# Unread matrix products in TensorE's estimated gaps, and new estimates for the order of a two-layer decoder

## The chip, the core and the metric

The kernel runs on one core of one Trainium2 chip. The metric is the device time of one execution in microseconds, the median of several. A core has five engines with an instruction stream each: TensorE (PE: matrix products and transposes), VectorE (DVE), ScalarE (ACT), GpSimd (POOL) and SyncE (SP, which only issues transfers here). Each works through its own stream in order and waits for the others through semaphores.

## The reference, cut to what matters

The input is `x`, 4 sequences of 256 tokens with 256 features: 1024 tokens in all. Six blocks are added to it in turn, each behind a layer normalisation:

```
x = x + L0_attn(norm(x))            # linear attention with a decay, 16 heads
x = x + L0_xattn(norm(x), itok, ctx)  # 4 experts chosen by token id, weights from ctx
x = x + L0_ffn(norm(x))             # product-key memory: 8 heads x 8 rows out of a table of 2048
x = x + L1_attn(norm(x))            # causal 3-tap convolution, attention inside blocks of 16, 8 heads
x = x + L1_xattn(norm(x), ctx)      # 16 heads over all 1024 context tokens, quantised to 8 bits
x = x + L1_ffn(norm(x))             # one shared and 16 routed experts, 2 for each token
```

In `L0_ffn` each token picks 64 rows of the table (8 heads of 8), forms a weight for each from the row's first 128 values, and adds the rows' other 256 values under these weights. In `L1_xattn` a softmax over 1024 keys is formed for every token and head and its probabilities are rounded to 8 bits.

## The kernel before

The tokens are 8 tiles of 128 (`xt[0]` to `xt[7]`). Work is written as Python generators, "streams", each of which yields the engine that it will need next. Their steps are woven into one order for TensorE, ScalarE and VectorE by hand-made estimates, while the program is built; on the chip nothing is decided any more.

- `Clock.note` (line 79) gives each instruction an estimated cost and keeps for each engine the time at which it is free. `Clock.weave` (line 111) takes, out of the streams that could start within `NEAR` = 0.6 us of the earliest, the one with the highest lead.
- `Slots` (line 155 on) counts PSUM buffers: `take` waits until one is free, `give` returns it. [...]In the first part `accs` has one bank and `f` (`bank`, line 348) seven; later `accs` has one, `sc` four (two buffers of two banks), `tp` one and `mm` two.

The streams are these.

- `front(b)`, b = 0 to 3 (pairs of tiles): the first three blocks up to the choice of table rows. Its products go into `f`.
- `fetches` (line 609): for each tile 8 steps of 8 indirect DMAs by GpSimd, which gather table rows into `g` (three buffers): 512 gathers.
- `weigh` (line 620): for each of the 64 steps, VectorE multiplies and sums `g`, ScalarE takes a tanh, VectorE writes the weights into `blk`, and TensorE adds the rows with 8 products of 32 columns into `accs[:, 0, :]`. When these are through, the buffer of `g` is free for the gathers three steps on.
- `locals_`: for each pair of tiles the fourth block and the queries of the fifth. `routes`: the router and the shared expert of the sixth. Both use `mm`.
- `units(k, 3)`, three streams at a time (line 943): the cross attention of one tile and head, 128 units in all. One unit is two products of 512 columns into `sc`, a maximum on VectorE, an exponential on ScalarE into 8-bit `e`, two transposes into `tp`, a cast on ScalarE from `tp` into `qqT`, and eight products of 16 columns into `accs[:, 1, :]` (`accs<-vi,qqT` in the profile).

After the weave come the routed experts (31 slots of 128 rows, lines 1195 to 1231) and the gathering of their results. That part is written without `Clock`.

All instructions that go through `Clock` stand in the profile under line 75, so they are told apart by the names of their tiles.

Of the kernel before, what the change touches and what calls it, by code (L numbers as in the profile page):

```python
# [11 lines left out]
F32 = mybir.dt.float32  # L12
BF16 = mybir.dt.bfloat16
# [8 lines left out]
P = 128  # L22
D = 256
# [28 lines left out]
class Clock:  # L52
# [26 lines left out]
    def note(self, engine, op, out, args, kw):  # L79
        if engine == "sync":  # L80
            return
        n = math.prod(out.shape[1:])
        if engine == "tensor":
            moved = args[2] if op == "matmul" else args[1]
            wide = moved.dtype == F32
            cost = 0.04 + n * ((0.0016 if op == "matmul" else 0.0022) if wide else 0.00085)
            if out.shape[0] == 32:
                cost = 0.115
        elif engine == "scalar":
            cost = 0.2 + n * 0.00083 + (0.2 if "accum_out" in kw else 0)  # L90
        elif engine == "gpsimd":
            cost = 1.25
        elif op in ("max", "max_index", "tensor_reduce"):
            src = args[1] if op != "max_index" else args[2]
            cost = 0.16 + 0.00104 * math.prod(src.shape[1:]) + (0.05 if op == "max_index" else 0)
        elif op == "reciprocal":
            cost = 0.1 + 0.0064 * n
        elif op == "tensor_tensor_scan":
            cost = 0.16 + 0.0022 * n
        else:  # L100
            cost = 0.16 + (0.00054 if op in ("tensor_scalar", "tensor_copy") else 0.00104) * n
        if self.last not in (None, engine):
            self.t = self.end + self.HOP
        start = max(self.free[engine], self.t)
        self.free[engine] = start + cost
        self.end = max(self.end, start + cost)
        self.last = engine
# [3 lines left out]
    def weave(self, streams):  # L111

        live = self.live = list(streams)
        while live:
            able = []
            for s in live:
                t = s.t
                engine, wait = s.wait  # L120
                if isinstance(wait, Slots):
                    if not wait.left:
                        continue
                    t = max(t, wait.at)
                elif wait is not None:
                    at = wait()
                    if at is None:
                        continue
                    t = max(t, at)
                able.append((max(t, self.free[engine]), t, s))  # L130
            first = min(x[0] for x in able)
            _, t, s = max((x for x in able if x[0] <= first + self.NEAR), key=lambda x: (x[2].lead, -x[1]))
            self.lead = s.lead
            self.t = self.end = t
            self.last = None
            try:
                s.wait = next(s.gen)
            except StopIteration:
                live.remove(s)
                s.done = self.end  # L140
            s.t = self.end + self.HOP

    def fork(self, *gens):

        made = [Stream(g, self.lead, self.end + self.HOP) for g in gens]
        self.live.extend(made)
        yield "vector", lambda: max(s.done for s in made) if all(s.done is not None for s in made) else None
# [8 lines left out]
class Slots:  # L156
# [7 lines left out]
    def take(self, shape, dtype=F32):  # L164
        while not self.left:
            yield "tensor", self
        self.left -= 1
        return self.pool.tile(shape, dtype, name=self.tag, tag=self.tag, bufs=self.n)

    def give(self):  # L170
# [4 lines left out]
def decoder(ctx, tc, a, out):  # L175


    nc = tc.nc
    ck = Clock(nc)
# [6 lines left out]
    A = SimpleNamespace(turned=None)  # L186
# [38 lines left out]
    ident = base.tile([P, P], F32, name="ident", tag="ident")  # L225
    make_identity(nc, ident)
    identb = base.tile([P, P], BF16, name="identb", tag="identb")
# [44 lines left out]
    psp = psum_ctx.enter_context(tc.tile_pool(name="psp", bufs=1, space=PSUM))  # L272
    psf = front_ctx.enter_context(tc.tile_pool(name="psf", bufs=1, space=PSUM))
# [2 lines left out]
    accs = psp.tile([P, 2, D], F32, name="accs", tag="accs")  # L276
    nc.vector.memset(accs, 0.0)

    blk = []
# [63 lines left out]

    hdram, pT, idxT, known = {}, {}, {}, {}
    fronts_left = [NB]
    bank = Slots(ck, psf, "f", 7)

    def front(b):  # L350
        tiles = (2 * b, 2 * b + 1)
# [591 lines left out]
    def units(k, n):  # L943

        work = A.work
        for j in range(k, NT * XH, n):
            t, h = j // XH, j % XH
            yield "tensor", lambda: qready.get(t)
            o, c = h % 2, h // 2
            hr = slice(o * 64, o * 64 + 64)  # L950
            psc = yield from A.sc.take([P, T])
            for n_ in range(2):
                te_.matmul(psc[:, n_ * 512:(n_ + 1) * 512], QT[t][hr, c, :], kT[hr, c, n_ * 512:(n_ + 1) * 512],
                           start=True, stop=True)
            yield "vector", None
            mx = work.tile([P, 1], F32, name="mx", tag="mx", bufs=4)
            ve_.tensor_reduce(mx, psc, AX.X, ALU.max)
            nb = work.tile([P, 1], F32, name="nb", tag="nb", bufs=4)
            ve_.tensor_scalar(nb, mx, NSQ[t][:, h:h + 1], ln255, ALU.mult, ALU.add)
            yield "scalar", None  # L960

            e = work.tile([P, T], U8, name="e", tag="e", bufs=3)
            se_.activation(e, psc, AF.Exp, bias=nb, scale=SQ[t][:, h:h + 1], accum_out=SUMS[t][:, h:h + 1])
            A.sc.give()
            yield "tensor", None

            tp = yield from A.tp.take([P, 2, P])
            for o in range(2):
                te_.transpose(tp[:, o, :], e.bitcast(F32)[:, o * P:(o + 1) * P], ident)
            yield "scalar", None  # L970
            qqT = work.tile([P, 8, P], BF16, name="qqT", tag="qqT", bufs=3)
            se_.copy(qqT.rearrange("p (o j) q -> p o j q", o=2), tp.bitcast(U8).rearrange("p o (q j) -> p o j q", j=4))
            A.tp.give()

            yield "tensor", lambda: 0.0 if t == 0 else summed.get(("o", t - 1))
            for s in range(NT):
                te_.matmul(accs[:, 1, h * XD:(h + 1) * XD], qqT[:, s, :], vi[:, s, h * XD:(h + 1) * XD],
                           start=False, stop=(s == NT - 1), skip_group_check=True)
            nunits[t] += 1
            if nunits[t] == XH:  # L980
                summed[("x", t)] = ck.end
# [147 lines left out]
    with tc.manual_schedule(engines={mybir.EngineType.PE, mybir.EngineType.Activation, mybir.EngineType.DVE}):  # L1129
        ck.weave([*[Stream(follow(b), 5.0 - b, (0.0, 20.0, 0.0, 0.0)[b]) for b in range(NB)],  # L1130
                  Stream(keys_values(), 0.5, 25.0), Stream(fetches(), 20.0), Stream(weigh(), 6.0),
                  Stream(turn()), Stream(weights()), Stream(locals_(), 1.5),
                  *[Stream(after_turn(units, k, 3), 2.0) for k in range(3)],
                  Stream(cross_out(), 3.0), Stream(routes(), 1.0)])
# [46 lines left out]
    for tj in range(NT * 2):  # L1181
# [3 lines left out]
                         start=(tj == 0), stop=(tj == NT * 2 - 1))  # L1185
# [115 lines left out]
def build(arrays):  # L1301
    import concourse.bacc as bacc

    nc = bacc.Bacc("TRN2", target_bir_lowering=False, num_devices=1)
    a = {k: nc.dram_tensor(f"in_{k}", v.shape, mybir.dt.from_np(v.dtype), kind="ExternalInput").ap()
         for k, v in arrays.items()}
    out = nc.dram_tensor("out_0", (T, D), F32, kind="ExternalOutput").ap()
    with tile.TileContext(nc) as tc, ExitStack() as ctx:
        decoder(ctx, tc, a, out)
    return nc  # L1310
# [9 lines left out]
```

## Time and profile before

| | us |
|---|---|
| three runs | 1367.18, 1361.3, 1358.31 (median 1361.3) |
| the profiled execution, whole | 1457.97 |
| its span, first to last instruction | 1456.2 |
| TensorE busy, granted clock over the span | 897.2 (62%), 0.659 |
| VectorE, ScalarE, GpSimd busy | 847.4, 519.3, 570.2 |
| first and last start of a gather (`g<-in_table`) | 126.4, 919.7 |
| first and last start of a unit's exponential (`e<-sc`) | 685.1, 1282.4 |

The profiled execution is 7% longer than the median of the runs, so times of the profile are set against its own span. "Clock" is the share of full speed that TensorE was granted. A busy time of TensorE is modelled, and work in flight overlaps. A row of the trace is one recorded instruction: an fp32 product leaves two of them, a bf16 product or an fp32 transpose one.

### The profile page before, as it was taken

How to read it: one execution, taken by the hardware profiler on the slowest of the kernel's cores; microseconds unless marked ns; L12 is line 12 of the kernel's file. 1: busy time of each engine (PE TensorE's matmuls, PEld its weight loads, DVE VectorE, ACT ScalarE, POOL GpSimd, SP SyncE). 2: the span in 40 equal slices, each digit the busy share in tenths (PEclk: the TensorE clock that was granted, in tenths of full speed). 3: DMA queues.
4: the chain of work that ended last, by engine and by line, in shares of the span. 5: the costliest groups of instructions: out<-in, count | busy, mean ns of one | idle time of the engine just before them, and what ended most of it. 6: DMA issues, size and time to landing. Idle time of an engine off the chain costs nothing.

```text
span 1456.2 us, 15280 instructions
## 1 busy us (share of the span) xinstructions
PE 897.2 (62%) x4829; PEld 530.4 (36%) x4829; DVE 847.4 (58%) x2309; ACT 519.3 (36%) x1039; POOL 570.2 (39%) x584
## 2 busy tenths in 40 slices
PE   4881561376624812645867664787679767756992
PEld 3670440154402500432333242444345443333551
DVE  6849476857775568246657557655654566533222
ACT  1341220122201301122555513668375838731220
POOL 1004676666667676646666656200000000002324
PEclk8995675588856855655655565755665565556996
DMA  5012577666667688855766657330000000003323
GB/s 173 0 34 75 145 172 179 163 172 171 179 180 181 175 243 216 198 147 142 179 170 173 166 152 176 100 124 0 8 0 0 1 8 1 1 8 73 89 71 102
DMA packets 93165, 165.56 MB, mean 114 GB/s; under 512 B 14858, under 2 KB 65275, under 8 KB 93084
## 3 DMA queue, kind: packets, MB, share of 16 engines
q0 software_dynamic: 35024, 106.86, 24.7%
q1 hardware_dynamic: 58060, 57.72, 18.7%
q8 instruction: 39, 0.64, 0.2%
q14 instruction: 42, 0.34, 0.1%
HBM read 157.85 MB, written 6.68 MB: 113 GB/s over the span
## 4 chain that ended last, share of the span: by engine, by line
PE 35%; DVE 25%; issue 15%; ACT 12%; DMA 5%; POOL 4%; another core or an unknown queue 3%; DVEq 0%; ACTq 0%; POOLq 0%
PE mm L75 11%; PE f L75 7%; PE accs L75 5%; ACT e L75 4%; ACT qqT L75 4%; POOL g L75 4%; DVE mx L75 3%; PE sc L75 3%; DMA g<-in_table,idxT 3%; PE ph L1211 3%; PE tp L75 3%; DVE g L75 2%; DVE z L75 2%; DVE oh L75 2%
## 5 line engine op out<-in xcount | busy, mean ns | idle before, releaser
L75 POOL DMA_INDIRECT g<-in_table,idxT x512 | 519.3, 1014 | 394.3 <-issue 146.9
L75 DVE TENSOR_REDUCE mx<-sc 128x1 f32<-128x1024 f32 x128 | 156.4, 1222 | 126.1 <-PE sc L75 107.3
L75 PE MATMUL accs<-g,blk 128*32 128x256 f32 x1024 | 110.6, 573 | 172.6 <-DVE blk L75 105.2
L1202 POOL DMA_INDIRECT xr<-xs,smap x31 | 29.3, 945 | 459.5 <-DVE smap L1189 402.4
L75 ACT ACTIVATE e<-sc,nb,qs_q 128x1024 uint8<-128x1024 f32 x128 | 154.2, 1205 | 69.5 <-DVE nb L75 62.2
L75 ACT CAST qqT<-tp 128x1024 bf16<-128x1024 uint8 x128 | 129.0, 1007 | 79.0 <-PE tp L75 56.9
L75 PE MATMUL sc<-kT,qT 64*128 64x512 bf16 x256 | 121.9, 585 | 31.0 <-ACT e L75 26.6
L75 PE MATMUL tp<-ident,e 128*128 128x128 f32 x256 | 83.4, 427 | 73.1 <-ACT qqT L75 45.0
L75 PEld LDWEIGHTS accs<-g,blk 128*32 128x32 f32 x1024 | 35.6, 147 | 225.2 <-DVE blk L75 120.8
L75 PEld LDWEIGHTS tp<-ident,e 128*128 128x128 f32 x256 | 35.8, 195 | 146.0 <-ACT qqT L75 75.9
L75 DVE TENSOR_TENSOR g<-g,hb 128x1024 f32<-128x1024 f32 x64 | 78.3, 1224 | 12.6 <-DMA g<-in_table,idxT 7.1
L75 DVE TENSOR_REDUCE z<-g 128x8 f32<-128x1024 f32 x64 | 78.1, 1220 | 3.0 <-issue 0.4
L75 PEld LDWEIGHTS <-qqT 128*128 128x128 bf16 x1024 | 48.2, 109 | 60.6 <-ACT qqT L75 32.5
L75 ACT ACTIVATE th<-u 128x8 f32<-128x8 f32 x64 | 13.3, 207 | 153.5 <-DVE u L75 85.4
L75 DVE SCALAR_TENSOR_TENSOR blk<-th,u 64x8 f32<-64x8 f32 x128 | 21.5, 168 | 69.1 <-ACT th L75 39.9
L75 PE MATMUL accs<-vi,qqT 128*128 128x16 bf16 x1024 | 49.7, 178 | 14.4 <-ACT qqT L75 8.6
L75 ACT ACTIVATE ln_xn<-x,ln_nmr,ln_rstd 128x256 f32<-128x256 f32 x48 | 26.3, 592 | 86.8 <-DVE ln_nmr L75 74.0
L1211 PE MATMUL ph<-w,xrT 128*128 x124 | 48.9, 507 | 0.7 <-DVE xrT L1208 0.6
L1215 DVE TENSOR_TENSOR hd<-hd,ph 128x176 f32<-128x176 f32 x31 | 10.4, 338 | 63.2 <-ACT hd L1214 63.2
L75 PE MATMUL f<-ident,ix 128*128 128x128 f32 x8 | 3.6, 450 | 64.6 <-DVE sm L75 51.4
L75 PE MATMUL f<-ident,ln_xn 128*128 128x128 f32 x48 | 12.1, 382 | 45.3 <-ACT ln_xn L75 18.5
L75 DVE TENSOR_SCALAR nb<-mx,nsq,ln 128x1 f32<-128x1 f32 x128 | 34.9, 273 | 8.4 <-DVE mx L75 0.5
(290 smaller groups left out, 1737.5 us busy)
## 6 DMA issues: line engine op xcount, KB each, us to landing
hb<-hdram SPq DMA_DIRECT2D x128, 256.0 KB
g<-in_table,idxT POOLq DMA_INDIRECT x512
w<-in_w SPq DMA_DIRECT2D x16, 352.0 KB
ys<-yr SPq DMA_DIRECT2D x31, 128.0 KB
w_w2a<-in_w SPq DMA_DIRECT2D x1, 2048.0 KB
x<-in_x SPq DMA_DIRECT2D x8, 128.0 KB
w_ctxT<-in_ctxT SPq DMA_DIRECT2D x1, 1024.0 KB
w_w_up<-in_w_up SPq DMA_DIRECT2D x1, 1024.0 KB
```

What stands on the lines that cost most here:

```text
L75: return emit(*args, **kw)
L1202: nc.gpsimd.indirect_dma_start(out=xr, out_offset=None, in_=xs, in_offset=bass.IndirectOffsetOnAxis(ap=smap[:, i:i + 1], axis=0))
L1211: nc.tensor.matmul(ph.rearrange("p j n -> p (j n)"), xrT[:, k, :], w13[:, bass.ds(e, 1), k, :], start=(k == 0), stop=(k == 1))
L1215: nc.vector.tensor_tensor(hd, hd, ph[:, 1, :], ALU.mult)
```

## The change

- The estimates for TensorE in `Clock.note` become smaller; an instruction of GpSimd is put at 1.3 instead of 1.25 us.
- A tile `spare`, one PSUM bank, is added beside `accs`. `keep_busy` is called before each step that begins on TensorE: where the estimated idle time of TensorE is over 0.3 us, it writes up to 24 products of 256 columns in bf16 (`identb` against `ident` read as bf16) into the first half of `spare`, one for each 0.16 us. They are not entered in the estimates. Nothing reads them.
- For this bank, `f` has six buffers instead of seven. Later the transposes of `e` go into the second half of `spare`; `take(None)` then only counts the one `tp` slot and makes no tile.

```diff
--- before.py
+++ after.py
@@ -83,13 +83,13 @@
         if engine == "tensor":
             moved = args[2] if op == "matmul" else args[1]
             wide = moved.dtype == F32
-            cost = 0.04 + n * ((0.0016 if op == "matmul" else 0.0022) if wide else 0.00085)
+            cost = max(0.14 if wide else 0.05, 0.03 + n * (0.0009 if wide else 0.00045))
             if out.shape[0] == 32:
-                cost = 0.115
+                cost = 0.08
         elif engine == "scalar":
             cost = 0.2 + n * 0.00083 + (0.2 if "accum_out" in kw else 0)
         elif engine == "gpsimd":
-            cost = 1.25
+            cost = 1.3
@@ -131,6 +131,8 @@
             first = min(x[0] for x in able)
             _, t, s = max((x for x in able if x[0] <= first + self.NEAR), key=lambda x: (x[2].lead, -x[1]))
             self.lead = s.lead
+            if s.wait[0] == "tensor":
+                self.keep_busy(max(t, self.free["tensor"]) - self.free["tensor"])
             self.t = self.end = t
             self.last = None
@@ -140,6 +142,15 @@
+    IDLE = 0.3
+    filler = None
+
+    def keep_busy(self, gap):
+
+        if self.filler is not None and gap > self.IDLE:
+            for _ in range(min(int((gap - 0.1) / 0.16), 24)):
+                self.filler()
+
@@ -165,6 +176,8 @@
         while not self.left:
             yield "tensor", self
         self.left -= 1
+        if shape is None:
+            return None
         return self.pool.tile(shape, dtype, name=self.tag, tag=self.tag, bufs=self.n)
@@ -275,6 +288,9 @@
     accs = psp.tile([P, 2, D], F32, name="accs", tag="accs")
     nc.vector.memset(accs, 0.0)
+
+    spare = psp.tile([P, 2, D], F32, name="spare", tag="spare")
+    ck.filler = lambda: nc.tensor.matmul(spare[:, 0, :], identb, ident.bitcast(BF16), start=True, stop=True)
@@ -345,7 +361,7 @@
-    bank = Slots(ck, psf, "f", 7)
+    bank = Slots(ck, psf, "f", 6)
@@ -964,7 +980,8 @@
-            tp = yield from A.tp.take([P, 2, P])
+            yield from A.tp.take(None)
+            tp = spare[:, 1, :].rearrange("p (o q) -> p o q", o=2)
             for o in range(2):
                 te_.transpose(tp[:, o, :], e.bitcast(F32)[:, o * P:(o + 1) * P], ident)
             yield "scalar", None
```

## The prediction

> **What bounds the kernel now.** I read the page first, then the busy time in six stretches, then the chain of waits, then single rows at both clocks.
>
> ```profile
> span 1456.2 us, 15280 instructions
> PE 897.2 (62%) x4829; PEld 530.4 (36%) x4829; DVE 847.4 (58%) x2309; ACT 519.3 (36%) x1039; POOL 570.2 (39%) x584
> PEclk8995675588856855655655565755665565556996
> PE 35%; DVE 25%; issue 15%; ACT 12%; DMA 5%; POOL 4%; another core or an unknown queue 3%; DVEq 0%; ACTq 0%; POOLq 0%
> ```
>
> No engine is full. TensorE holds the largest share of the chain (35%), and its clock sits at five to six tenths from slice 12 to slice 34. A faster clock is worth something only in that 35%.
>
> ```profile
> 0.00:137.00 137.00, 79.55 (x354) 64.15 (x354) 97.73 (x355) 36.98 (x74) 14.67 (x33) 0.84 0.21 65
> 137.00:600.00 463.00, 222.35 (x1263) 142.37 (x1263) 304.77 (x971) 81.60 (x194) 312.01 (x306) 0.67 0.72 183
> 600.00:921.00 321.00, 199.29 (x1224) 105.60 (x1224) 188.59 (x382) 129.18 (x261) 199.08 (x198) 0.58 0.64 162
> 921.00:1296.00 375.00, 283.39 (x1572) 154.87 (x1568) 207.60 (x429) 241.50 (x409) 0.00 (x0) 0.58 0.06 20
> 1328.00:1456.00 128.00, 96.99 (x368) 54.48 (x368) 34.15 (x108) 26.61 (x93) 40.61 (x43) 0.87 0.31 86
> ```
>
> The columns are the busy times of PE, PEld, DVE, ACT and POOL, then the clock, the DMA share and GB/s. I call the first four stretches A (fronts before the gathers), B and C (gathers, with fronts, then with attention), D (attention after the last gather). In B and C GpSimd paces: a gather takes 0.95 us and 0.30 us of issue, so 512 need 640 of the 784 us from 137 to 921. Of the rest, the view of `accs` puts 79.7 us down to buffers that TensorE frees late. In D TensorE is the fullest engine (283 of 375 us, against 242 for ScalarE), and the chain of that window says the same:
>
> ```profile
>   POOL g L75: 79.7, 21
> by line: PE mm L75 26.2%; ACT e L75 13.3%; ACT qqT L75 12.9%; PE sc L75 8.7%; PE tp L75 8.0%; DVE mx L75 6.1%; issue 5.1%; PE accs L75 3.0%; DVE q L75 1.7%; DVE ln_nt L75 1.4%; DVE nb L75 1.4%; ACT pr L75 1.3%; DVE x L75 1.1%; DVE ln_st L75
> ```
>
> The same work at both clocks (start, length, engine, operation), half clock first:
>
> ```profile
> 149.01 1.94 PE L75 MATMUL accs<-g,blk 128*32 128x256 f32 x16 [5.16 <-DVE blk L75]
> 928.79 1.07 PE L75 MATMUL accs<-g,blk 128*32 128x256 f32 x16
> 970.14 1.03 PE L75 MATMUL sc<-kT,qT 64*128 64x512 bf16 x2
> 921.05 0.59 PE L75 MATMUL sc<-kT,qT 64*128 64x512 bf16 x2
> 975.41 0.69 PE L75 MATMUL tp<-ident,e 128*128 128x128 f32 x2
> 927.10 0.44 PE L75 MATMUL tp<-ident,e 128*128 128x128 f32 x2
> ```
>
> Doubling the clock K takes these to 0.55 to 0.64 of their time; a unit's eight `accs<-vi,qqT` stay near 0.4 us. I write TensorE's time as proportional to 0.2 + 0.4/K: 0.89 at K = 0.58, 0.83 at 0.63, 0.77 at 0.7, 0.67 at 0.85, 0.6 at 1.
>
> **What the Trainium skill says.** "TensorE: Matmul & The Clock Gate", Part 1, says that the array runs at half clock unless it was busy for a window of about 3.4 us. The trace agrees: every stretch that I took out had 1.00 or 0.50 and nothing between, in multiples of 3.4 us. The same page, "Back-to-back issue gap", prices a bf16 product of N columns at N/1.2 ns cold and N/2.4 + 2.5 ns warm. So one added product is put at 213 ns cold and 109 ns warm, 0.126 us at K = 0.85, an estimate from that page; the trace has no such product. "PSUM — Partial Sum Buffer", Terms, says that two engines must not use the same bank at once. No run here shows a collision, but it matters for `spare`, where the added products and the casts' source share a bank.
>
> **What counts as busy.** From 960 to 1000 us TensorE is busy 31.1 of 40 us and the clock is 0.50; from 40 to 80 us it is busy 32.4 and the clock is 0.96. So busy time alone doesn't decide. I tallied columns streamed in each 3.4 us window (fp32 records twice; products on 64 rows half, on 32 columns a quarter, `accs<-vi,qqT` nothing, weights chosen to fit which windows are followed by full clock). Full speed follows about 4000 from cold, and stays above about 3400. Stretch means: A 3950 (clock 0.84), B 2650 (0.67), C 2210 (0.58), D 2300 (0.58), 1296 to 1440 us 4060 (0.85).
>
> **The change, part by part.**
>
> The order of TensorE's instructions after the change has 2622 added products in 284 runs: 286 before the first `accs<-g`, 1070 from there to the first `sc`, 667 from there to the last `accs<-g`, 599 behind it. Over the 1160 us from 137 to 1296 that is 2336 products, 598,000 columns, or 1760 in each 3.4 us. With it the means become 4410 in B, 3970 in C and 4060 in D. By A and the tail, such means go with about 0.85. I take K = 0.85 in B, C and D.
>
> The new estimates move work. At the last `accs<-g` the order before has emitted 45 units and 261 products or transposes into `mm`; the order after 64 and 335. So 19 units and 74 `mm` instructions leave D for B and C, where ScalarE was free (129 of 321 us in C).
>
> D: TensorE keeps 64 of 83 units and 215 of 290 `mm` instructions, about 76% of its work: 283 x 0.76 = 215 us. At K = 0.85, x 0.67/0.89 = 162. Added: 599 x 0.126 = 75. Sum 237. At today's filling (283/375 = 0.755) D lasts 314 us: 61 us less.
>
> A flaw keeps D from being shorter. In 98 runs (544 products) the first added product carries a wait for ScalarE: it shares the bank that the cast to `qqT` reads. 56 of them stand ahead of `accs<-vi,qqT` and 38 ahead of the next transposes, which need that same cast too. There the added products fill no gap; they start when the work behind them could start, 5.6 (544/98) x 0.126 = 0.7 us each. That is why I leave the filling at 0.755 and don't raise it.
>
> B and C: TensorE had 222 + 199 = 421 us. It takes over 19 units at 2.1 us (1.03 + 0.69 + 0.41) = 40, and 74 x 0.45 (131 us for 290 `mm` instructions in D) = 33: 494 us. At K = 0.85, x 0.67/0.83 = 399. Added: 1737 x 0.126 = 219. Sum 618 of 784 us: 79% full instead of 54%. Its products for `weigh` come behind more, and on these GpSimd waits. Of the added ones 831 stand in 58 runs straight ahead of `accs<-g`: 14.3 each, 1.8 us. Where TensorE waited for `blk` (26 groups, 105 us, 4 us each) they fit. In the other 38 they delay: 68 us, of which a third reaches GpSimd, as today 21 of 64 do: +23. The faster groups themselves (1.94 to about 1.2 us, 64 times, a third) give back 15. The third part, fuller queues, is not in the trace; between -10 and +60, taken as +12. B and C: +20 us.
>
> A: 286 products, mostly ahead of transposes that wait for a layer normalisation, and a clock already at 0.84: 0, from -5 to +10. Six buffers of `f` instead of seven: 0 to +10, taken as 0, since TensorE's own speed frees them sooner. TensorE's program grows by 2622 loads and 2622 products; ScalarE once waits 16.1 us for an unknown queue in B, which may be instructions; 0 to +15, taken as 0. The tail is untouched at 0.87.
>
> Sum: -61 + 20 = -41 on 1457.97, so 1417. The median of the runs stands at 1361.3/1457.97 = 0.934 of the profiled execution: -38, so 1323 us.
>
> **The rivals.**
>
> Full effect: K = 1 in D and the gathers at their own pace. D: 215 x 0.6/0.89 + 599 x 0.109 = 210, /0.755 = 278, 97 less; B and C 10 less. -107 x 0.934: 1261 us. For it: full clock persists once 3400 columns are kept up. Against: the runs are bursts, and TensorE's waits for `blk` last up to 17 us.
>
> The gathers give it back: as D shrinks by 61, B and C grow by 60, because 79% filling in order delays most `accs<-g`. For it: 79.7 us of waits are there already. Against: GpSimd has three buffers. 1361 us.
>
> Slower: the clock stays near 0.7, because bursts of 4 to 7 products don't fill a window, and the added products become load instead of warmth. 0.155 us each. B and C: 494 x 0.77/0.83 + 1737 x 0.155 = 727 of 784 us, 93% in order; the gathers stretch by some 50. D: 215 x 0.77/0.89 + 599 x 0.155 = 279, /0.755 = 369, nothing gained. +50 x 0.934: 1408 us. It decides from K below about 0.77, where D's gain (some 30 us) no longer covers the gathers' loss. For it: the threshold from cold is nearly a full window. This is also the case in which the change doesn't do what it says.
>
> **How the numbers follow.** Forecast 0.42 (1323; alone 1295 to 1347), full effect 0.13, given back 0.20, slower 0.25. Below 1270 lies half of the full effect; above 1410 nearly half of the slower case; so 1270 to 1410. About 1% is what a measurement of this kernel can tell. Faster by over 1%: nearly all of the forecast, the full effect, a fifth of the given-back case: 0.57. Within 1%: three fifths of that case, a little of its neighbours: 0.16. Slower: 0.27.
>
> **What would show it.** The clock should read about 0.85 from 137 us on and the mean over the span over 0.8; at 0.7 the slower case holds. The last gather should start near 940 us, with about 60 exponentials before it; over 970 means that it was given back. The stretch from the last gather to the end of the units should last near 315 us. In it `accs<-vi,qqT` should wait behind added products after the cast. A span near 1415 us fits; over 1475 it is wrong.

## The result: slower by 6.6%, and the gathers end 98 us later

| | before | after |
|---|---|---|
| median of the runs, us | 1362.5 | 1453.0 |
| ratio, 95% interval | | 1.066 (1.0625 to 1.070) |
| profiled execution: span, clock | 1364.3, 0.665 (second profile) | 1452.6, 0.804 |

The forecast was 1323 us, range 1270 to 1410: it expected a gain, and the time came out above the range. Ratios leave out executions over 1.5% longer than the fastest of their kernel; medians hold all of them.

First a correction to what the prediction stood on. Its profile of the kernel before (span 1456.2) is of an execution that the runs don't resemble. A second profile of the same kernel has a span of 1364.3 us, and from here on "before" means that one. The two differ in one place: the last gather starts at 920 us in the first and at 826 in the second; from there to the first read of the routed experts (`xr`) it is 403 and 405 us, behind it 133 and 133.

The page after: TensorE busier, its clock up, as wished. The lines are the span, the engines' busy times and the clock in 40 slices.

```profile
span 1452.6 us, 20511 instructions
PE 1138.4 (78%) x7451; PEld 757.6 (52%) x7451; DVE 846.0 (58%) x2309; ACT 524.9 (36%) x1039; POOL 575.1 (40%) x584
PEclk8997998999997879756598978885656855577996
```

Busy time by stretch, cut at the last gather and at the first `xr`; columns PE, PEld, DVE, ACT, POOL, clock, DMA share, GB/s. Before (second profile), then after:

```profile
0.00:137.00 137.00, 79.58 (x354) 64.07 (x354) 97.59 (x355) 36.98 (x74) 14.67 (x33) 0.84 0.22 65
137.00:600.00 463.00, 244.74 (x1454) 156.36 (x1454) 333.68 (x1030) 97.92 (x246) 351.72 (x339) 0.68 0.81 201
600.00:826.00 226.00, 161.95 (x1037) 82.24 (x1034) 161.65 (x326) 115.24 (x210) 164.57 (x166) 0.58 0.75 192
826.00:1231.00 405.00, 300.48 (x1617) 165.86 (x1616) 220.75 (x490) 243.47 (x417) 0.60 (x1) 0.57 0.07 21
1231.00:1364.00 133.00, 98.09 (x372) 54.88 (x372) 34.78 (x110) 27.72 (x94) 44.46 (x47) 0.86 0.31 86
```

```profile
0.00:137.00 137.00, 105.13 (x576) 86.39 (x577) 95.32 (x351) 37.30 (x74) 14.49 (x33) 0.88 0.21 65
137.00:600.00 463.00, 369.81 (x2662) 269.21 (x2661) 344.09 (x1059) 112.01 (x264) 336.05 (x323) 0.89 0.76 193
600.00:924.00 324.00, 257.95 (x1910) 156.48 (x1909) 191.78 (x359) 160.09 (x294) 179.05 (x182) 0.77 0.58 147
924.00:1320.00 396.00, 307.93 (x1937) 190.85 (x1934) 180.14 (x434) 188.05 (x316) 1.12 (x1) 0.68 0.08 21
1320.00:1452.00 132.00, 97.55 (x372) 54.68 (x372) 34.72 (x109) 27.48 (x94) 44.39 (x47) 0.87 0.31 86
```

The gathers end 98 us later; the attention behind them is only 9 us shorter although it holds 65 units instead of 88; nothing else moves. Of the 98 us, 84 fall on the last three of the eight tiles of gathers, while attention units are under way: these tiles take 134, 104 and 107 us, where before they took 85, 85 and 91. GpSimd's waits for buffers that TensorE frees (view of `accs`, us and times) went from the first line to the second:

```profile
  POOL g L75: 14.3, 11
  POOL g L75: 106.2, 26
```

In the attention the added products stand where they hurt. From the timeline after (start, length; in brackets the idle time before and what ended it):

```profile
999.53 1.01 ACT L75 CAST qqT<-spare 128x1024 bf16<-128x1024 uint8 x1 [0.98 <-PE spare L75]
...
1000.59 1.23 PE L293 MATMUL spare<-ident,identb 128*128 128x256 bf16 x5 [1.16 <-ACT qqT L75]
...
1001.61 0.63 PE L75 MATMUL spare<-ident,e 128*128 128x128 f32 x2
...
1002.04 1.06 PE L293 MATMUL spare<-ident,identb 128*128 128x256 bf16 x4
...
1002.89 0.40 PE L75 MATMUL accs<-vi,qqT 128*128 128x16 bf16 x8
1003.13 1.01 ACT L75 CAST qqT<-spare 128x1024 bf16<-128x1024 uint8 x1 [1.28 <-PE spare L293]
...
1003.23 1.03 PE L75 MATMUL sc<-kT,qT 64*128 64x512 bf16 x2
...
1004.30 1.23 DVE L75 TENSOR_REDUCE mx<-sc 128x1 f32<-128x1024 f32 x1 [3.84 <-PE sc L75]
```

The cast (`CAST`) reads the second half of `spare`, and the added products write its first half. TensorE sits idle for 1.16 us while the cast runs, the very gap that the five products were meant for. They start when the cast has ended, and the next transposes wait behind them. Four more follow these; the next cast reads the same bank and starts at 1003.13, when they are through. The next `sc` is late, and VectorE has been idle for 3.84 us. `spare` is one tile and one bank, so no run here tells for which of the two the wait is placed; below, both are called the bank.

### The profile page after: what moved, and what is told of

Same layout as the page of the kernel before. It is cut to its first block, busy times and chain, and to the rows that moved or that the text cites. A ratio compares the mean times of both kernels' runs of the same rounds, so it can differ in the third digit from the quotient of the medians.

```text
span 1452.6 us, 20511 instructions
## 1 busy us (share of the span) xinstructions
PE 1138.4 (78%) x7451; PEld 757.6 (52%) x7451; DVE 846.0 (58%) x2309; ACT 524.9 (36%) x1039; POOL 575.1 (40%) x584
## 5 line engine op out<-in xcount | busy, mean ns | idle before, releaser
L293 PE MATMUL spare<-ident,identb 128*128 128x256 bf16 x2622 | 418.2, 317 | 116.0 <-ACT qqT L75 114.1
L293 PEld LDWEIGHTS <-identb 128*128 128x128 bf16 x2622 | 288.0, 112 | 227.2 <-issue 162.9
L75 ACT CAST qqT<-spare 128x1024 bf16<-128x1024 uint8 x128 | 129.3, 1010 | 163.5 <-PE spare L75 142.4
L75 PE MATMUL accs<-g,blk 128*32 128x256 f32 x1024 | 83.5, 453 | 54.7 <-DVE blk L75 54.6
L75 PE MATMUL sc<-kT,qT 64*128 64x512 bf16 x256 | 104.7, 513 | 7.4 <-ACT e L75 7.2
L75 PEld LDWEIGHTS accs<-g,blk 128*32 128x32 f32 x1024 | 30.1, 123 | 89.7 <-DVE blk L75 63.2
L75 PE MATMUL spare<-ident,e 128*128 128x128 f32 x256 | 72.8, 379 | 3.3 <-ACT qqT L75 2.9
L75 PEld LDWEIGHTS spare<-ident,e 128*128 128x128 f32 x256 | 37.8, 184 | 57.5 <-issue 39.9
```

Source lines behind the costliest of these rows:

```text
L75: return emit(*args, **kw)
L293: ck.filler = lambda: nc.tensor.matmul(spare[:, 0, :], identb, ident.bitcast(BF16), start=True, stop=True)
```

## The experiments

All are read by their medians and by the ratio to the kernel before on the same chip. The first twelve ran on chips where that takes 1362 to 1365 us, the last six on chips where it takes 1464 to 1466; times of the two sets are not compared by microseconds.

### The kernel before, again

No edit.

> The kernel before, unchanged, for a profile of an execution that lasts as long as its timed runs (its first profile was 7% longer than they are). Theory A (the first profile was an unusual execution, with long waits for an unknown queue during the gathers): the span is near 1362 us, the last gather starts near 830 us instead of 920, and the clock is near 0.66. Theory B (the timed runs have a warmer TensorE): the span is near 1362 us with a clock of 0.75 or more. Theory C: the profile lengthens this program, and the span is near 1456 us again with timed runs near 1362.

1363.8 us; span 1364.3, clock 0.665, last gather at 826 us, and no waits for an unknown queue: theory A. The eight tiles of gathers take 85 to 91 us each, where the first profile had 95 to 108.

### No products

```diff
-    IDLE = 0.3
+    IDLE = 1e9
```

> The changed kernel with IDLE at 1e9, so that no added product is emitted; new estimates, spare and six buffers of f stay, and all other instructions stand in the same order. Theory P (the added products are load, and half of them stand behind the cast that the next work waits for): the loss of 91 us goes with them, 1340 to 1370 us. Theory O (the order from the small estimates is at fault): it stays slow, 1420 us or more. Theory W (the warmth pays and the order costs even more): slower still than 1453 us.

1383.2 us, ratio 1.017 (1.0115 to 1.022). Between the theories: the order alone, with six buffers of `f`, costs 21 us, the products the other 70. The stretch of the gathers and the attention behind it:

```profile
137.00:897.00 760.00, 473.98 (x2842) 275.47 (x2842) 537.13 (x1416) 272.70 (x560) 511.87 (x503) 0.64 0.73 180
897.00:1249.00 352.00, 227.19 (x1271) 122.81 (x1271) 178.40 (x429) 184.89 (x312) 0.86 (x2) 0.58 0.09 24
```

The gathers end 71 us later than before (826 to 897) and the rest up to the first `xr` is 53 us shorter (405 to 352). The gathers stretch although TensorE is busy for only 474 of 760 us. GpSimd's waits for buffers that TensorE frees:

```profile
  POOL g L75: 90.0, 33
```

### Products, but the old estimates

```diff
-            cost = max(0.14 if wide else 0.05, 0.03 + n * (0.0009 if wide else 0.00045))
+            cost = 0.04 + n * ((0.0016 if op == "matmul" else 0.0022) if wide else 0.00085)
...
-                cost = 0.08
+                cost = 0.115
...
-            cost = 1.3
+            cost = 1.25
```

> The changed kernel with the estimates of before, so that the order of all else is that of before; 1710 added products instead of 2622, in the gaps of the old estimates. Theory P: the loss falls with the number of products, some 60 us over before, near 1420 us. Theory O: the loss goes, 1340 to 1370 us.

1385.2 us, ratio 1.020 (1.014 to 1.025). Neither figure was met. In this order 43 runs with 232 products wait for a cast, where the changed kernel has 98; shared out, the 23 us of loss are 0.5 us for each of the 43.

### No products in the time of the cast

```diff
-        if self.filler is not None and gap > self.IDLE:
+        if self.filler is not None and gap > self.IDLE and self.casting is None:
...
                 te_.transpose(tp[:, o, :], e.bitcast(F32)[:, o * P:(o + 1) * P], ident)
+            ck.casting = j
...
+            if ck.casting == j:
+                ck.casting = None
             nunits[t] += 1
```

> The changed kernel, but no products are added between a unit's two transposes and its eight products behind the cast, so that none waits for ScalarE: 1970 instead of 2622 are left. Theory P in its form that the shared bank costs (each such run delays the chain by some 0.7 us and drags the cast): 60 us or more come back, below 1395 us. If the products cost only as load, a quarter of the loss goes, about 1430 us. Theory O: no change, 1453 us.

Here `casting` holds a unit from its two transposes until its eight products behind the cast; 652 of the 2622 products go. 1383.1 us, ratio 1.017 (1.012 to 1.023): 70 us come back, to the time without any product. So the products of the cast's time cost 70 us, and the other 1970 together nothing on balance. In the lines below the gathers end at 892 instead of 924 us and the attention takes 351 instead of 396.

```profile
137.00:892.00 755.00, 604.25 (x4261) 395.69 (x4258) 536.52 (x1414) 273.00 (x559) 512.78 (x503) 0.81 0.71 181
892.00:1243.00 351.00, 256.76 (x1578) 147.61 (x1578) 178.50 (x429) 184.39 (x312) 0.82 (x2) 0.64 0.09 25
```

Beside the kernel without products the clock is up from 0.64 to 0.81 where GpSimd's gathers and their waits set the time, but only from 0.58 to 0.64 in the attention, where TensorE's speed was expected to count.

### The old estimates, and no products in the time of the cast

The edits of the last two together.

> The estimates of before (the order of all other instructions is that of before) with 1448 added products, none between a unit's transposes and its products behind the cast. Theory P (only the products behind the cast cost; the rest is free): the 23 us that the old order with 1710 products lost come back, 1355 to 1365 us. If the warmer clock pays at all in this order: below 1350 us, faster than both kernels. Theory L (every added product costs as load): 1375 us or more.

1361.6 us, ratio 0.999 (0.997 to 1.001), clock 0.760. The 23 us are back, and 1448 products change nothing: gathers 84 to 90 us a tile, 402 us of attention at a clock of 0.62.

### One product in the time of the cast

```diff
-            for _ in range(min(int((gap - 0.1) / 0.16), 24)):
+            for _ in range(min(int((gap - 0.1) / 0.16), 24 if self.casting is None else 1)):
```

> The changed kernel, but between a unit's transposes and its products behind the cast a run has one added product instead of four or more: 2098 in all, 98 runs still wait for the cast. If the work of these products costs (some 0.7 us for each run on the path): most of the 70 us comes back, 1385 to 1405 us. If the wait that they carry is what costs: 1440 us or more.

`casting` is set as in "No products in the time of the cast". 1393.3 us, ratio 1.023 (1.018 to 1.028). The 98 waits are still there and cost about 10 us with one product each. It is the work started after the wait that costs: from the first product of such a run to the next other work of TensorE it is 96.0 us in all in the changed kernel, and 15.9 here.

### A bank for each, against a shared one

```diff
-        A.mm = Slots(ck, A.ps, "mm", 2)
+        A.mm = Slots(ck, A.ps, "mm", 1)
...
-            yield from A.tp.take(None)
-            tp = spare[:, 1, :].rearrange("p (o q) -> p o q", o=2)
+            tp = yield from A.tp.take([P, 2, P])
```

The first hunk alone makes the shared kernel, both make the one with a bank for each. Both have 2794 products in the same places.

> One buffer of mm instead of two frees a bank: the transposes of e go back to a bank of their own and the added products (2794, also those of the time of the cast) have theirs. Read only against the next kernel, which has the same order of instructions. Theory P: 60 us or more below it, since the products then run while the cast runs. If the products cost as load alone: within 15 us of it.

> One buffer of mm instead of two, all else as in the changed kernel: transposes and added products share a bank, 95 runs wait for the cast. With one buffer of mm slower than 1453 us. Theory P: 60 us or more above the kernel with a bank for each; load alone: within 15 us of it.

A bank for each: 1370.7 us, ratio 1.004 (1.002 to 1.0055). Shared: 1463.3 us, ratio 1.072 (1.067 to 1.077). The same products in the same order cost 93 us more for the bank alone. With two buffers of `mm`, as in the changed kernel, no bank is left for this, so there it was not tried. Who waits for the tile `spare` (us, times), shared, then own; the transposes write `spare` only in the shared kernel, so the last line gives the casts' waits for `tp` in the other:

```profile
  ACT qqT L75: 145.7, 95
  PE spare L293: 103.5, 85
```

```profile
  PEld f L75: 2.4, 2
  POOL g L75: 0.6, 2
```

```profile
  ACT qqT L75: 76.9, 69
```

The products' own waits for the cast are gone, and the casts wait about half as long.

### A bank for each, without products

On top of both hunks:

```diff
-    IDLE = 0.3
+    IDLE = 1e9
```

> The kernel with one buffer of mm and a bank for each, without any added product, in the same order: what the warmer clock is worth. If warmth pays: 20 to 50 us above the 1371 us of the kernel with 2794 products. If it doesn't: within 10 us of it.

1440.7 us, ratio 1.055 (1.051 to 1.059): products with a bank of their own are worth 70 us in this order. The two stretches without products, then with them:

```profile
137.00:896.00 759.00, 467.63 (x2728) 269.48 (x2728) 518.75 (x1391) 252.32 (x513) 515.65 (x503) 0.64 0.73 180
896.00:1306.00 410.00, 276.09 (x1386) 144.18 (x1385) 196.30 (x453) 205.53 (x359) 0.72 (x1) 0.52 0.07 21
```

```profile
137.00:862.00 725.00, 594.45 (x4550) 407.12 (x4549) 522.20 (x1394) 252.59 (x514) 507.21 (x502) 0.90 0.76 188
862.00:1237.00 375.00, 309.77 (x2127) 195.48 (x2125) 192.63 (x451) 204.13 (x357) 1.19 (x2) 0.79 0.08 23
```

Half of it (34 us) comes ahead of the last gather, half (35) behind it; there the clock goes from 0.52 to 0.79. So here a warmer clock pays, also ahead of the last gather, where with two buffers of `mm` it didn't; why is not shown. The order with one buffer of `mm` takes the gain back: without products it is some 55 us slower than the order with two (1440.7 against 1383.2), which is itself 21 us slower than before.

### A bank for each, with the old estimates

> Products in a bank of their own (one buffer of mm), with the estimates of before: 1959 products, none waits for a cast. If the order from the new estimates is what keeps the kernel with a bank for each at 1371 us: faster than before, 1330 to 1350 us. If gathers set the pace and warmth has nothing left to give: 1355 to 1370 us.

1393.3 us, ratio 1.021 (1.018 to 1.024): both theories missed. The gathers run at full pace (83 to 91 us a tile, last one at 819 us), but only 34 units are started by then, and the rest takes 436 us with one buffer of `mm`.

### One estimate at a time

The kernel before with only GpSimd's estimate changed (1.25 to 1.3), and with only TensorE's.

> The kernel before with only the estimate of a GpSimd instruction changed, 1.25 to 1.3 us (54 instead of 45 units ahead of the last weighing). The new estimates together cost 21 us. If work pulled ahead of the weighing is what delays the gathers: about half of that, 1370 to 1378 us, with the last gather 20 to 40 us later. If the estimates of TensorE are what matters: 1362 us.

> The kernel before with only TensorE's estimates changed (61 units ahead of the last weighing), two buffers of mm, seven of f, no spare. If pulled work is what delays: most of the 21 us, 1375 to 1385 us, with the last gather 40 us or more later. If the GpSimd estimate or the lost buffer of f is what matters: 1362 us.

GpSimd's alone: 1336.3 us, ratio 0.978 (0.974 to 0.981): faster than both kernels, and not as expected. TensorE's alone: 1363.0 us, ratio 0.999 (0.997 to 1.001). A line of the trade for each order, all without products:

| order | last gather, us | units started by then | from there to the first `xr`, us | median, us |
|---|---|---|---|---|
| before | 826 | 40 | 405 | 1362 |
| GpSimd's estimate | 832 | 49 | 374 | 1336 |
| TensorE's estimates | 862 | 53 | 370 | 1363 |
| both (six buffers of `f`) | 897 | 63 | 352 | 1383 |

In these four orders, the more units stand ahead of the last gather, the shorter the rest. Nine more than before come nearly free for the gathers (7 us); with 13 and 23 more they pay 36 and 71 us, as much as the rest saves and more. The orders differ in more than this count, so it is a fit of four points and not shown as the cause.

### What the other chips left open

These six runs are three kernels, each run twice, on chips where the kernel before takes 1464 to 1466 us. The first is the kernel with the old estimates and no products in the time of the cast, with GpSimd's estimate at 1.3. The second is the kernel before with all new estimates and nothing else. The third is the kernel with a bank for each, without products in the time of the cast.

> GpSimd's estimate at 1.3 us, TensorE's estimates of before, and 1433 added products of which none stands between a unit's transposes and its products behind the cast. The estimate alone gave 1336 us. If products outside the cast's time are neutral, as they were twice: 1330 to 1342 us. If warmth pays in this order: below 1330 us. If they cost as load: above 1345 us.

> The same kernel as e13 (GpSimd's estimate at 1.3 us, 1433 products, none during a cast), on a chip of the usual speed if it falls so. Products neutral: 1330 to 1342 us, as GpSimd's estimate alone (1336). Warmth pays: below 1330. Load: above 1345. On the slow chip: 0.985 to 0.995 of before, as e13.

0.990 (0.9845 to 0.995) and 0.992 (0.990 to 0.995), slightly faster than before here too; the medians of all runs, 1457.7 and 1455.4 us, are 0.994 of before. Whether the products add to GpSimd's estimate or take from it isn't shown, since that estimate alone ran on no such chip.

> The kernel before with all new estimates and nothing else: seven buffers of f, no spare, no products. The same order as the changed kernel without products (1383 us), which has six buffers of f. If the lost buffer of f costs the 21 us: 1360 to 1366 us. If the two estimates together make the worse order: 1378 to 1388 us, with the last gather near 895 us.

> The same kernel as e14 (all new estimates on the kernel before, seven buffers of f). If the lost buffer of f costs the 21 us: 1360 to 1366 us. If the two estimates together make the worse order, for which the 1.009 of the slow chip speaks: 1375 to 1388 us, with the last gather near 895 us.

1.0087 (1.006 to 1.012) and 1.009 (1.0055 to 1.013): slower with seven buffers of `f`. So the two estimates together make the worse order; whether the lost buffer adds to the 21 us stays open.

> One buffer of mm, a bank for each, 2202 products: those of the time of the cast are left out (2794 with them gave 1371 us, none at all 1441 us). If the products during the cast are what keeps the clock up in the attention: 1400 to 1440 us, with the clock after the last gather falling from 0.79 to about 0.65. If with one buffer of mm any warmth pays: within 15 us of 1371 us.

> The same kernel as e15 (one buffer of mm, a bank for each, no products during a cast). If the products during the cast carry the clock in the attention: 1400 to 1440 us, for which its clock of 0.68 after the last gather on the slow chip speaks. If any warmth pays: within 15 us of 1371 us.

1.037 (1.033 to 1.040) and 1.046 (1.041 to 1.051). The stretch behind the last gather in the first and the second:

```profile
1016.00:1400.00 384.00, 284.63 (x1802) 161.58 (x1801) 195.87 (x453) 205.40 (x359) 1.06 (x2) 0.68 0.08 23
998.00:1385.00 387.00, 288.32 (x1814) 163.25 (x1813) 195.99 (x453) 205.65 (x359) 0.59 (x1) 0.68 0.08 22
```

This stretch differs little between the two sorts of chip (403 and 405 us in the two profiles of before), so it may be set beside the other two kernels of this order: 410 us and clock 0.52 without products, 375 us and 0.79 with all. By that, the products outside the casts bring 23 to 26 of the 35 us, and those in the time of the cast the rest and the step from 0.68 to 0.79. It is one comparison across chips and no proof.

## Why the prediction was wrong, by its own steps

- **The gathers: the step that failed first.** "B and C: +20 us." The whole change stretched them by 98 us, and the new order alone, without one added product, by 71. The term of the sum that was too small is "fuller queues", "between -10 and +60, taken as +12". It was the only place for what the moved work does to the weighing, and this came out above the whole range. In the kernel without products GpSimd's waits for buffers grew from 14.3 to 90.0 us, 64.9 of them in the last three tiles of gathers. TensorE was not full there (474 of 760 us), so its fullness was the wrong measure. Which engine's order holds the weighing up isn't shown: in those tiles VectorE also waits 26.7 us for ScalarE's tanh. The +23 us for products ahead of `accs<-g` did not show: with the products outside the casts the gathers end at 892 us, without any at 897.
- **The room in the first profile.** Its stretch of 784 us held 79.7 us of waits, where an execution like the timed ones has 689 us and 14.3. The forecast of TensorE's load was good (618 us, measured 628), but in 689 us that would have been 90% full, not 79%.
- **The shared bank: named, and put at nothing.** The prediction saw the 98 runs that wait for the cast and priced them at 0.7 us each, but they entered the sum only as a filling not raised above 0.755, in D. Measured: 70 us for the products of the cast's time. Of the 76 us between the two profiled spans 45.7 fell in D and 31.5 in the gathers. Shared out over the runs this is 0.71 us, and that it meets 0.7 is in part luck: each run held up TensorE's next work by 0.98 us in the mean (96.0 in 98 runs), and not all of this reached the end. It also left out that the next cast waits in turn for products emitted ahead of it.
- **The order.** Forecast: D shrinks by 61 us, from the order, the clock and the added products together. The new order alone shortened it by 53 us at an unchanged clock. That the two are near is luck: by the prediction's own figures the order alone gives 375 - 215/0.755 = 90. The unit count (64 of 128 ahead of the last weighing) came out as 63 started.
- **The clock.** Forecast: 0.85 from 137 to 1296 us, over 0.8 in the mean. Measured 0.89 and 0.77 in the gathers, 0.68 behind them, 0.804 in the mean: right for the first part, too high for the last, where it was to pay. The sum spread the 2336 products evenly, 1760 columns in each 3.4 us; by its own count only 599 of them stand in D, about 1400, and D also gives away a quarter of its own columns. Counted as the prediction does, by the start of each record, B, C and D had 5200, 3600 and 3100 columns, not 4410, 3970 and 4060. The threshold of 4000 from cold doesn't come out of such a count either. In both profiles of before, the one after and the one with a bank for each, up to the first `xr`, half clock followed 689 of the 698 windows of 3.4 us with under 2800 columns, and full clock 566 of the 578 with 3600 or more, with the clock at half or at full alike; in between it went either way.
- **The price of a product.** Forecast 0.126 us. TensorE was busy with them for 418.2 us, 0.160 each, but this holds the modelled end of the last one of each of the 284 runs. From start to start within a run it was 0.139 us in the mean, and from 0.109 in the median to 0.213 for the slow tenth: the two prices that the prediction had taken.
- **The scale.** The factor 0.934 spread the 7% of the first profile over all stages. The second profile has all of it in the gathers.
- **The rivals.** "The gathers give it back" had the right place, at +60 where the order alone made +71, and no price for the bank on top. "Slower" named a clock near 0.7 and products that are only load. In D the clock was 0.68, but that is not what cost: without the products of the cast's time it was 0.64 there, and D was 45 us shorter.
- **The signs.** Three that it named for its forecast came true in a kernel that was 6.6% slower: a mean clock over 0.8 (0.804), a last gather near 940 us (923) and about 60 exponentials before it (63). They stood on the first profile's scale; against the second the gathers ended 98 us late. The end of the units did tell: 360 us behind the last gather, not 315.

The loss of 91 us is thus 21 for the order with six buffers of `f` (71 lost in the gathers, 53 won back, by the profiles), nothing on balance for the products outside the casts, and 70 for those in the time of the cast. That they cost because they share its bank is shown with one buffer of `mm`, where the same products with a bank of their own cost nothing and brought 70 us; for the changed kernel itself the waits in its trace say the same.

## What to carry to other kernels

Work that is to fill a gap must not depend on what ends the gap: give it a buffer and a bank that no other engine is reading, or leave it out there. A warmer clock is no gain in itself: from 0.67 to 0.76 or 0.78 in the mean it bought nothing twice here, and in one other order, from 0.65 to 0.87, it bought 70 us. Look at the stage where others wait for TensorE, not at the mean. Before a number is taken from a profile as slack, set the profile's span against the timed runs, and if they differ find the stage that does. And set signs of success on the scale of the timed runs.

## What was not expected of the hardware

The kernel before took 1362 to 1365 us on some chips and 1464 to 1466 on others. In the first profile and in all six taken on chips of the second sort engines wait for an unknown queue (`remote` in the view of waits), 108 to 198 us in all; in the thirteen other profiles there is no such wait. In the first profile the gathers take 95 to 108 us a tile instead of 85 to 91, and its execution took 1458 us. That fits with its having been taken on such a chip, though the record doesn't name its chip. What differs between the chips was not tried.
